# Expert layers of a four-layer kernel: gate maximum and difference in the step of the transposes, gates in seven steps

## Chip, cores and metric

The kernel runs on 1 core of one Trainium2 chip. The metric is the device time of one execution in microseconds (us), lower is better. Before the change it is 4801.95 us, the median of 3 runs (4800.6 to 4808.87).

## What is computed

A tensor of 4 images with 128 channels and 64 x 64 positions passes four layers: a deformable convolution, a state-space block, a layer of attention and feed-forward with experts behind it, and a second attention, again with experts behind it. The change touches the experts alone, which occur twice with the same code. Seen as tokens, the input is 16,384 rows of 128 numbers; each row chooses 2 of 8 experts:

```python
def _ln_t(v, eps=1e-5):
    m = jnp.mean(v, axis=-1, keepdims=True)
    s = jnp.var(v, axis=-1, keepdims=True)
    return (v - m) / jnp.sqrt(s + eps)

def _L2_ffn_ref(x, router_w, router_b, expert_w, expert_b):
    B, N, D, C, E, K = (8, 8192, 128, 128, 8, 2)
    router_probs = jax.nn.softmax(x @ router_w + router_b, axis=-1)
    top_p, top_i = jax.lax.top_k(router_probs, K)
    top_p = top_p / jnp.sum(top_p, axis=-1, keepdims=True)
    expert_out = jnp.einsum('bnd,edc->bnec', x, expert_w) + expert_b
    gathered = jnp.take_along_axis(expert_out, top_i[..., None], axis=2)
    return jnp.einsum('bnk,bnkc->bnc', top_p, gathered)

t = t + _L2_ffn_ref(_ln_t(t), ...)     # layer 2, behind its attention
...
t = t + _L3_ffn_ref(_ln_t(t), ...)     # layer 3, the same with other weights
x = _from_tokens(t, x)
```

The kernel computes all 8 experts for every row and weighs them with a gate that is zero for 6 of the 8.

## The kernel before

`moe(layer)` (line 2063) is one expert layer. All 16,384 rows lie in SBUF as `X`, seen as `T`: 128 tiles of 128 rows by 128 channels. The tiles are taken in nine groups, `SIZES = [8, 8] + [16] * 7`. A group passes four stages, each written as a generator that stops at a `yield` after each step:

- `moments(i)` (line 2101): one BN_STATS on VectorE per tile into the PSUM tile `w`, then seven small operations on `odd`, `rstd` and `w`; ScalarE makes `rstd` from them by Ln and Exp; VectorE makes `mean`.
- `logits(i)` (line 2126): ScalarE writes the normalised tiles `v`; four at a time are transposed by TensorE into the PSUM bank `psv`, copied by ScalarE into `vT`, and multiplied by the router weights into `psl`; at the end ScalarE copies `psl` into `lT`.
- `gates(i)` (line 2157): TensorE transposes `lT` into the PSUM bank `psg` (four transposes); VectorE takes the maximum `m` over the 8 logits of a row and writes the difference into `both`; ScalarE takes Exp of `both`; VectorE does the rest on `both`, `w` (the work space for `pr` and `one`), `mx`, `rk`, `m` and ends with `gate`. In the profile the parts of this rest are: "m<-both, reciprocal, w<-both,w, mx<-w" (four operations), twice "w<-w,mx; w<-w,rank; rk<-w; w<-w,rk" (four operations each, called the match below), between them "gate<-w; w<-w,gate; both<-w,mx; mx<-w" (the removal), and at the end five operations that end with `gate<-w,m`.
- `experts(i, s)` (line 2210), one pair of tiles per call: per tile two products of TensorE into two banks `pex` (four per pair; the profile counts each as two passes), scaled by the gate and added up. In even slots ScalarE scales three experts per tile and VectorE the other five (`x<-pex,gate` and `x<-pex,gate,x`); in odd slots ScalarE scales four and VectorE four (`x<-pex,gate`, 128 x 512). GpSimd adds what is left (`x<-x`) and adds the sum onto `X`.

`flip(q)` (line 2235), in layer 3 alone, transposes four finished tiles by TensorE into the bank `psf`, ScalarE copies them into `o`, and SP's queue sends `o` to the output.

`psv`, `psg` and `psf` share one PSUM buffer: the pool `pv` has `bufs=1` and all three have `tag="psv"`. `pex` has five buffers, `x` three.

The rounds `p = -3 ... 8` (line 2247) run the four stages in a skewed way: round `p` computes the experts of group `p` in slots of one pair, and beside it the gates of `p+1`, the logits of `p+2` and the moments of `p+3`. Rounds -3 to -1 have no experts and 12 slots, rounds 0 and 1 have 4 slots, rounds 2 to 8 have 8. In each slot `experts` is issued first, then in layer 3 after each second pair a `flip`, then steps of the gates, the logits and the moments, in that order, as many as the share of the round that has passed asks for:

```python
for step, i in ((gates, p + 1), (logits, p + 2), (moments, p + 3)):
    if 0 <= i < N:
        parts = {gates: 8, logits: SIZES[i] // 2 + 2, moments: SIZES[i] // 4 + 3}[step]
        beside.append([step(i), parts, 0])
...
    for a in beside:
        while a[2] < -(-a[1] * (s + 1) // slots):
            next(a[0])
            a[2] += 1
```

`moe` issues through `InOrder`, which holds every engine to this order of the program; every instruction issued through it carries line 85 in the profile. With 8 slots, one gates step falls on each slot. With 4 slots, two fall on each. With 16 tiles in a group of the logits and 8 slots, the first four `v` are written in slot 0, the first transposes into `psv` come in slot 1.

Of the kernel before, what the change touches and what calls it, by code (L numbers as in the profile page):

```python
# [94 lines left out]
class Kernel:  # L95
# [1967 lines left out]
    def moe(self, layer):  # L2063
# [6 lines left out]
        SIZES = [8, 8] + [16] * 7  # L2070
        T = self.X.rearrange("p (t c) -> p t c", c=P)
        LAST = P - 1
        with ExitStack() as ctx:
# [83 lines left out]
            def gates(i):  # L2157
                n = SIZES[i]
                vT, lT = st.pop(("logits", i))
                ps = pv.tile([P, 4, 4, 32], F32, name="psg", tag="psv")  # L2160
                for k in range(4):
                    nc.tensor.transpose(ps[:, k].rearrange("p j e -> p (j e)"), lT[:, k * P:(k + 1) * P], self.ident)
                quads = [P, n // 4, 4, NE]
                sh = [P, n, NE]
                psl = ps[:, :, 0:n // 4, 0:NE].rearrange("p k j e -> p j k e")

                def across(x):
                    return x.unsqueeze(2).to_broadcast(sh)

                yield  # L2170

                pr, one = (work[name][:, 0:n] for name in ("pr", "one"))
                both = sm.tile(sh, F32, name=f"both{n}")
                gate = sm.tile(sh, F32, name=f"gate{n}")
                m = sm.tile([P, n], F32, name=f"m{n}")
                mq = m.rearrange("p (j k) -> p j k", k=4)
                nc.vector.tensor_reduce(mq, psl, AX.X, ALU.max)
                nc.vector.tensor_tensor(both.rearrange("p (j k) e -> p j k e", k=4), psl,
                                        mq.unsqueeze(3).to_broadcast(quads), ALU.subtract)
                yield  # L2180
                nc.scalar.activation(both, both, AF.Exp)
                yield
                nc.vector.tensor_reduce(m, both, AX.X, ALU.add)
                nc.vector.reciprocal(work["m"][:, 0:n], m)
                nc.vector.tensor_tensor(pr, both, across(work["m"][:, 0:n]), ALU.mult)

                mx = sm.tile([P, n, 2], F32, name=f"mx{n}")
                rk = sm.tile([P, n], F32, name=f"rk{n}")
                for k in range(2):
                    nc.vector.tensor_reduce(mx[:, :, k], pr, AX.X, ALU.max)  # L2190
                    yield
                    nc.vector.tensor_tensor(one, pr, across(mx[:, :, k]), ALU.is_equal)
                    nc.vector.tensor_tensor(one, one, rank.unsqueeze(1).to_broadcast(sh), ALU.mult)
                    nc.vector.tensor_reduce(rk, one, AX.X, ALU.max)
                    nc.vector.tensor_tensor(one, one, across(rk), ALU.is_equal)
                    yield
                    if k == 0:
                        nc.vector.tensor_scalar(gate, one, -2.0, None, ALU.mult)
                        nc.vector.tensor_add(pr, pr, gate)
                        nc.vector.tensor_tensor(both, one, across(mx[:, :, 0]), ALU.mult)  # L2200
                    else:
                        nc.vector.tensor_tensor(one, one, across(mx[:, :, 1]), ALU.mult)
                        nc.vector.tensor_add(one, one, both)
                nc.vector.tensor_reduce(m, mx, AX.X, ALU.add)
                nc.vector.reciprocal(m, m)
                nc.vector.tensor_tensor(gate, one, across(m), ALU.mult)
                st["gates", i] = vT, gate
                yield

            def experts(i, s):  # L2210
                vT, gate = st["gates", i]
                t0 = first[i] + 2 * s
                x = xp.tile([P, 2, NE, P], F32, name="x")
                at_once = s % 2 == 0
                for u in range(2):
                    k = 2 * s + u
                    pex = [pe.tile([P, 4, P], F32, name="pex") for h in range(2)]
                    for h in range(2):
                        nc.tensor.matmul(pex[h], vT[:, k, :], ew[:, 512 * h:512 * (h + 1)], start=True, stop=True)
                    for e in range(3 if at_once else 4):  # L2220
                        nc.scalar.activation(x[:, u, e, :], pex[0][:, e, :], AF.Identity, scale=gate[:, k, e:e + 1])
                    if at_once:
                        nc.vector.tensor_scalar(x[:, u, 3, :], pex[0][:, 3, :], gate[:, k, 3:4], None, ALU.mult)
                        for e in range(4):
                            nc.vector.scalar_tensor_tensor(x[:, u, e, :], pex[1][:, e, :],
                                                           gate[:, k, 4 + e:5 + e], x[:, u, e, :],
                                                           ALU.mult, ALU.add)
                    else:
                        nc.vector.tensor_tensor(x[:, u, 4:NE, :], pex[1],
                                                gate[:, k, 4:NE].unsqueeze(2).to_broadcast([P, 4, P]), ALU.mult)  # L2230
                for w in (2, 1) if at_once else (4, 2, 1):
                    nc.gpsimd.tensor_tensor(x[:, :, 0:w, :], x[:, :, 0:w, :], x[:, :, w:2 * w, :], ALU.add)
                nc.gpsimd.tensor_tensor(T[:, t0:t0 + 2, :], T[:, t0:t0 + 2, :], x[:, :, 0, :], ALU.add)

            def flip(q):

                ps = pv.tile([P, 512], F32, name="psf", tag="psv")
                for k in range(4):
                    nc.tensor.transpose(ps[:, k * P:(k + 1) * P], T[:, 4 * q + k, :], self.ident)
                o = xp.tile([P, 512], F32, name="o")  # L2240
                nc.scalar.copy(o, ps)
                n, q = divmod(q, L // 512)
                nc.sync.dma_start(self.out[n][:, q * 512:(q + 1) * 512], o)
# [3 lines left out]
            for p in range(-3, N):  # L2247

                beside = []
                for step, i in ((gates, p + 1), (logits, p + 2), (moments, p + 3)):  # L2250
                    if 0 <= i < N:
                        parts = {gates: 8, logits: SIZES[i] // 2 + 2, moments: SIZES[i] // 4 + 3}[step]
                        beside.append([step(i), parts, 0])
                slots = SIZES[p] // 2 if p >= 0 else 12
                for s in range(slots):
                    if p >= 0:
                        experts(p, s)
                        pairs += 1
                        if layer == 3 and pairs % 2 == 0 and pairs >= 6:
                            flip(pairs // 2 - 3)  # L2260
# [5 lines that stand above are left out]
                    assert next(a[0], None) is None and a[2] == a[1]  # L2266
# [705 lines left out]
```

## Time and profile before

| view | value |
|---|---|
| profiled execution, its own time | 4802.76 us |
| span of that execution | 4800.9 us |
| median of the 3 runs | 4801.95 us |
| busy share of the span: PE, DVE, ACT, POOL | 92%, 71%, 75%, 65% |
| experts of layer 2, first BN_STATS to last add onto `X` | 2196.91 to 2513.5 us |
| experts of layer 3, first BN_STATS to the end | 4458.26 to 4800.9 us |
| 2340 to 2360 us (layer 2, a middle round): PE, DVE, ACT, POOL busy of 20 us | 18.60, 15.34, 14.30, 18.25 |
| 4620 to 4640 us (layer 3, a middle round): the same | 17.93, 14.77, 14.51, 16.13 |
| 2200 to 2220 us and 4460 to 4480 us (starts): PE busy of 20 us, granted clock | 13.67 at 0.50; 12.34 at 0.53 |
| a round of 8 slots, from one `psg` to the next | 34.69 us in layer 2, 37.38 us in layer 3 |

A line of the timeline gives start, duration, engine, operation, what it writes and reads, how many instructions were merged, and in brackets how long the engine had been idle before and what ended that. Times are from the start of the span. The whole kernel has 67,063 instructions; the two expert layers take 317 and 343 us of it.

### The profile page before, as it was taken

The page shows a single profiled execution, that of the slowest core. Times are in us where ns is not written, and L with a number is a line of the kernel's source. Part 1 is how long each engine was busy: PE and PEld are TensorE (multiplying, and loading weights), DVE is VectorE, ACT ScalarE, POOL GpSimd, SP SyncE. Part 2 cuts the span into 40 slices and gives each one's busy share as a digit, 9 for nine tenths or more (in the row PEclk, how much of TensorE's full clock was granted, in tenths as well). Part 3 has the DMA queues.
Part 4 walks back from the last instruction along what each step waited for, and adds up shares of the span by engine and source line. Part 5 has one row for each costly group of instructions (what it writes and reads, how often), then busy time and mean ns, then how long its engine had stood idle before and what let it go on. Part 6 is the DMA issues. An engine that isn't in the chain of part 4 may idle for free. (4 is left out here: it accounts for less than half of the span.)

```text
span 4800.9 us, 67063 instructions
## 1 busy us (share of the span) xinstructions
PE 4424.1 (92%) x23064; PEld 2411.2 (50%) x23064; DVE 3391.4 (71%) x6475; ACT 3618.5 (75%) x5498; POOL 3117.7 (65%) x3443
## 2 busy tenths in 40 slices
PE   6889987899997899997989999999999999999798
PEld 4778775566774344443434444444444444444344
DVE  5999996666645888855866666766676666665675
ACT  4456553566666777775758999999999999999575
POOL 0234443367783455544887878887888788877488
PEclk9999999999998999998999999999999999999899
DMA  6666773101002000000000000000000000000000
GB/s 213 186 184 188 194 193 82 26 22 30 28 17 90 23 1 1 0 1 1 36 36 1 1 1 1 1 1 1 1 1 1 1 1 1 1 1 1 10 29 34
DMA packets 71704, 196.33 MB, mean 41 GB/s; under 512 B 13940, under 2 KB 17204, under 8 KB 69684
## 3 DMA queue, kind: packets, MB, share of 16 engines
q1 hardware_dynamic: 65924, 175.96, 12.8%
q0 software_dynamic: 2240, 12.85, 1.0%
q8 instruction: 187, 3.06, 0.3%
q10 hardware_dynamic: 3184, 3.08, 0.2%
q14 instruction: 169, 1.38, 0.1%
HBM read 133.23 MB, written 50.74 MB: 38 GB/s over the span
## 5 line engine op out<-in xcount | busy, mean ns | idle before, releaser
L85 POOL TENSOR_TENSOR r<-r 128x512 f32<-128x512 f32 (+1 forms) x1088 | 1348.7, 1241 | 332.4 <-DVE r L85 271.8
L85 DVE TENSOR_TENSOR r<-r,num 128x1024 f32<-128x1024 f32 (+1 forms) x1088 | 975.4, 928 | 599.6 <-PE num L85 495.2
L85 PE MATMUL D<-F,G 32*128 32x512 f32 (+3 forms) x4608 | 1139.2, 573 | 2.1 <-DVE den L85 0.9
L85 PE MATMUL num<-F,G 32*128 32x512 f32 (+3 forms) x4608 | 1057.2, 590 | 6.8 <-DVE r L85 3.9
L85 ACT ACTIVATE r<-r 128x2048 f32<-128x2048 f32 (+4 forms) x610 | 1018.5, 1679 | 51.3 <-POOL r L85 4.7
L85 ACT ACTIVATE r<-D 128x1536 f32<-128x1536 f32 (+1 forms) x544 | 763.6, 1404 | 49.8 <-PE D L85 29.6
L85 PEld LDWEIGHTS D<-F,G 32*128 32x128 f32 x4608 | 484.2, 184 | 373.6 <-issue 235.1
L85 PE MATMUL acc<-r,v 128*128 128x512 f32 (+3 forms) x1152 | 598.1, 606 | 0.7 <-ACT r L85 0.7
L85 POOL TENSOR_TENSOR x<-x 128x512 f32<-128x512 f32 (+2 forms) x320 | 405.4, 1267 | 148.4 <-DVE m L85 66.5
L85 PEld LDWEIGHTS num<-F,G 32*128 32x128 f32 x4608 | 383.3, 183 | 223.4 <-issue 110.7
L85 PE MATMUL pff<-hid,w_ffn_w2T 128*128 128x512 f32 x1024 | 468.6, 600 | 0.0
L85 PE MATMUL pex<-w_expert_w,vT 128*128 128x512 f32 x1024 | 461.4, 598 | 1.6 <-DVE x L85 1.4
L85 POOL TENSOR_TENSOR piece<-v,wt 128x512 f32<-128x512 f32 x160 | 167.6, 1065 | 376.2 <-DVE cum L85 90.0
L85 PEld LDWEIGHTS acc<-r,v 128*128 128x128 f32 x1152 | 174.1, 188 | 382.7 <-issue 180.4
L85 PE MATMUL acc<-ident,pr 128*128 128x128 f32 x2560 | 319.1, 282 | 45.2 <-DVE pr L85 45.2
L85 ACT ACTIVATE x<-pex,gate 128x128 f32<-128x128 f32 x896 | 257.5, 368 | 102.2 <-PE pex L85 76.9
L85 PEld LDWEIGHTS acc<-ident,pr 128*128 128x128 f32 x2560 | 296.0, 146 | 59.9 <-DVE pr L85 58.6
L85 ACT ACTIVATE hid<-phh,cols 128x512 f32<-128x512 f32 x416 | 253.1, 689 | 67.7 <-PE phh L85 67.7
L85 PEld LDWEIGHTS pex<-w_expert_w,vT 128*128 128x128 f32 x1024 | 190.6, 192 | 216.5 <-issue 160.6
L85 PEld LDWEIGHTS pff<-hid,w_ffn_w2T 128*128 128x128 f32 x1024 | 185.0, 191 | 200.9 <-issue 200.9
L85 DVE TENSOR_TENSOR pr<-v,near_w 128x2560 f32<-128x2560 f32 x96 | 270.2, 2815 | 6.2 <-PE acc L85 5.4
L85 DVE SCALAR_TENSOR_TENSOR cop<-lp,cols,cop 128x512 f32<-128x512 f32 x192 | 143.4, 747 | 35.5 <-ACT cop L85 33.4
(502 smaller groups left out, 7656.6 us busy)
## 6 DMA issues: line engine op xcount, KB each, us to landing
v<-tab SPq DMA_DIRECT2D x320, 256.0 KB
oms<-omw SPq DMA_DIRECT2D x32, 432.0 KB
omr<-oms SPq DMA_DIRECT2D x32, 432.0 KB
X<-in_x_dram SPq DMA_DIRECT2D x8, 1024.0 KB
tab<-vb SPq DMA_DIRECT2D x64, 128.0 KB
o<-o SPq DMA_DIRECT2D x32, 256.0 KB
oin<-o SPq DMA_DIRECT2D x32, 256.0 KB
kept<-X SPq DMA_DIRECT2D x4, 2048.0 KB
```

The source lines that it names most:

```text
L85: self.last = op(*args, **kwargs)
```

## The change

The first `yield` of `gates` goes, the one between the transposes into `psg` and the tiles of the next step. The first step of the gates now issues the four transposes, the maximum and the difference; the second is the Exp, and so on, seven steps in all. The number in the table of parts is set to 7.

```diff
@@ -2167,8 +2167,6 @@
                 def across(x):
                     return x.unsqueeze(2).to_broadcast(sh)
 
-                yield
-
                 pr, one = (work[name][:, 0:n] for name in ("pr", "one"))
                 both = sm.tile(sh, F32, name=f"both{n}")
                 gate = sm.tile(sh, F32, name=f"gate{n}")
@@ -2249,7 +2247,7 @@
                 beside = []
                 for step, i in ((gates, p + 1), (logits, p + 2), (moments, p + 3)):
                     if 0 <= i < N:
-                        parts = {gates: 8, logits: SIZES[i] // 2 + 2, moments: SIZES[i] // 4 + 3}[step]
+                        parts = {gates: 7, logits: SIZES[i] // 2 + 2, moments: SIZES[i] // 4 + 3}[step]
                         beside.append([step(i), parts, 0])
                 slots = SIZES[p] // 2 if p >= 0 else 12
                 for s in range(slots):
```

No instruction is added or removed. With 8 slots the seven steps fall on slots 0 to 6, one each. With 4 slots two fall on each of the slots 0 to 2 and one on slot 3. With 12 slots they fall on slots 0, 1, 3, 5, 6, 8 and 10, where the eight steps fell on 0, 1, 3, 4, 6, 7, 9 and 10.

## Prediction

> **What bounds the kernel now.** First the engines' shares of the span: PE is busy for 92%, and in the middle rounds of both expert layers for 18 of 20 us, so there the question is what makes PE pause. The chain of waits of layer 3 tells it (start, duration, what the end hung on):
>
> ```profile
> 4616.80 3.45 PE pex L85 x8
> ...
> 4620.27 0.69 DVE x L85
> 4620.96 0.21 DVE m L85
> ...
> 4621.19 0.30 DVE both L85
> ...
> 4621.63 0.65 PE psf L85 x4
> ```
>
> The chain leaves PE for one scaling, the maximum and the difference. PE's timeline shows why, here for layer 3 and, in the last line, layer 2:
>
> ```profile
> 4616.19 0.60 PE L85 MATMUL psg<-ident,lT 128*128 128x128 f32 x4
> 4616.63 3.60 PE L85 MATMUL pex<-w_expert_w,vT 128*128 128x512 f32 x8
> 4621.63 0.63 PE L85 MATMUL psf<-ident,X 128*128 128x128 f32 x4 [1.40 <-DVE both L85]
> 4622.94 0.66 PE L85 MATMUL psv<-ident,v 128*128 128x128 f32 x4 [0.68 <-ACT o L85]
> ...
> 2313.39 0.63 PE L85 MATMUL psv<-ident,v 128*128 128x128 f32 x4 [1.40 <-DVE both L85]
> ```
>
> `psf` (layer 3) or `psv` (layer 2) wants the one buffer that holds `psg` until DVE has read it in slot 1, behind slot 1's scaling. This happens five times in layer 2 (rounds 2 to 6; round 7 has no logits) and six times in layer 3 (rounds 2 to 7), always 1.40 us.
>
> Then what lies close behind PE: POOL's timeline in an 8-slot round of layer 2, and its last pauses in each layer.
>
> ```profile
> 2319.03 2.07 POOL L85 TENSOR_TENSOR x<-x 128x512 f32<-128x512 f32 x2 [0.87 <-DVE x L85]
> ...
> 2331.22 4.50 POOL L85 TENSOR_TENSOR x<-x 128x1024 f32<-128x1024 f32 x3 [1.15 <-DVE x L85]
> ...
> 4739.37 2.07 POOL L85 TENSOR_TENSOR x<-x 128x512 f32<-128x512 f32 x2 [0.85 <-DVE x L85]
> ```
>
> POOL has 0.87 + 1.15 = 2.0 us to spare in a round of 34.69 us. Last the timelines of DVE, ACT and PE in the starts and the rounds of 4 slots, whose order the change also moves:
>
> ```profile
> 4468.03 1.31 DVE L85 BATCH_NORM_STATS2 w<-X 128x6 f32<-128x128 f32 x4
> 4473.38 0.23 DVE L85 TENSOR_REDUCE m<-psg 128x8 f32<-128x64 f32 x1 [4.05 <-PE psg L85]
> 4484.06 0.22 DVE L85 TENSOR_TENSOR gate<-w,m 128x64 f32<-128x64 f32 x1
> 4484.38 1.66 ACT L85 ACTIVATE x<-pex,gate 128x128 f32<-128x128 f32 x6 [2.32 <-PE psg L85]
> 4488.51 0.63 PE L85 MATMUL psv<-ident,v 128*128 128x128 f32 x4 [4.13 <-DVE both L85]
> 4488.97 5.29 PE L85 MATMUL pex<-w_expert_w,vT 128*128 128x512 f32 x8
> ...
> 2241.10 0.31 ACT L85 ACTIVATE rstd<-rstd,eps 128x16 f32<-128x16 f32 x1 [1.41 <-DVE rstd L85]
> 2244.25 1.13 PE L85 MATMUL psl<-vT,rws 128*128 128x512 f32 x2 [2.00 <-ACT vT L85]
> ```
>
> Both lie on the path: at the start PE waits 4.13 us for what hangs on `gate`, and at the end of a 4-slot round PE waits 2.00 us for a chain DVE statistics, ACT `rstd`, `v`, `vT`.
>
> **The 8-slot rounds: the gain.** The maximum and difference move to slot 0, behind slot 0's scalings. In layer 3 DVE's work of slot 0 ends at 4617.74 and `psg` is there at 4616.79: no new wait. The buffer is free while PE does the 3.60 us of slot 1, so all pauses go: 11 x 1.40 = 15.4 us. The copy of `o` (0.68) still holds `psv` once.
>
> What is late next: POOL. In layer 2 its spare 2.0 us takes the 1.40 of each round, except that in round 2 slot 5's `x` comes only 0.6 us earlier and POOL passes on the other 0.8; POOL's last pause (1.15 us at 2435.28) is used up and it runs through to the end. In layer 3 its last pause is the 0.85 us of the fence above, against 1.40: 0.55 is given back. Net gain 15.4 - 0.8 - 0.55 = 14.05.
>
> The rest of the gates come one slot earlier each, over the same instructions: four operations (1.25 us) go into slot 2, the match (four operations, 1.32) out of slot 7. PE gets its `pex` banks back from DVE later in between; the tightest bank has 0.65 us left by my replay of slot 6. I cost it at nothing; if that cover is gone, a pause as long as the lost one comes back.
>
> **The starts: four statistics.** In round -1 four BN_STATS lie ahead of `m<-psg`, inside its wait of 4.05 us. They now come behind it, and DVE then runs without a pause up to `gate`, so `gate` comes 1.31 us later, in two layers: +2.6. The bounds are 0 (another pause takes them) and 3.0 (Exp ahead of two `v` adds 0.2 each).
>
> **Slot 0 of the 4-slot rounds: Exp ahead of the four `v`.** Two gates steps fall on a slot. Before they were transposes and maximum; now maximum and Exp. ACT's Exp waits for DVE's `both`, and the four `v` (1.66 for four) queue behind it on ACT. `psv` needs both the buffer and the `v`; before, the `v` were written during the wait for `both`. So if `both` ends at B, the next `pex` started at B + 0.61 (0.14 from the chain, 0.47 from `psv` to `pex` in the fence). Now the Exp (I take 0.31, as for the small ACT operation `rstd`) and the four `v` (1.66) come first, each transposed as it is written, and some 0.13 for the last: B + 2.1. That is +1.5 in each of four rounds, 6.0, less 0.57 in layer 3 round 1, where `m<-both` waited so long for the Exp: +5.4. Bounds: 0 if the chain at the end of the round keeps its time, 4 x 1.97 = 7.9 if Exp and `v` come wholly on top.
>
> **Slots 0 to 3 of the same rounds: one match more ahead of the statistics.** The seven small operations that lead to `rstd` stand behind the gates' steps in DVE's queue. With seven steps one more match is ahead of them: 4 x 0.26 = 1.05 (128 x 64) in round 0, 1.32 (128 x 128) in round 1. The chain behind it (Ln and Exp, `x` of slot 3, `vT`, `psl`, the next round's `psg`) moves by it: 2 x 2.37 = +4.7. Bounds 0 to 4.7.
>
> Sum of the losses 2.6 + 5.4 + 4.7 = 12.7 (12.8 unrounded); with the gain, -1.3.
>
> **The granted clock.** Pauses cost more than their length. After 4.13 us PE's next eight passes took 5.29 instead of 3.60: 1.7 us for one stretch at half clock. It also came after 2.64 + 0.68 us (1.06 + 0.48 = 1.54), and once out of eleven after 1.40 + 0.68:
>
> ```profile
> 4546.99 8.73 PE L85 MATMUL pex<-w_expert_w,vT 128*128 128x512 f32 x16
> ```
>
> where five other rounds show 7.03. It did not come after 1.88, 2.00, 1.71 and 2.73. The change lengthens six such pauses of rounds 0 and 1: in slot 0 1.88, 1.71 and 1.72 to some 3.2 to 3.75, in slot 3 2.00, 1.99 and 2.73 to some 3.05, 3.04 and 4.05. I take half of them slow, 3 x 1.7 = 5.1, and drop the stretch of 4546.99, whose first pause goes: +3.4. Bounds: none slow, -1.7; all slow, 10.2 - 1.7 = +8.5.
>
> [...]
>
> **The sum.** The profiled execution took 4802.76 us (span 4800.9 and 1.86 around it), 0.8 above the median of the runs. 4802.76 - 14.05 + 12.8 + 3.4 = 4804.9, less 0.8: 4804. With the clock's bounds and half of the uncertain losses it is 4797 to 4811.
>
> **Rivals.**
>
> A, faster. The gain is paid eleven times from measured pauses; the losses are argued. If the ends of the 4-slot rounds absorb all that slot 0 and the starts lose, only the gain is left: 4801.95 - 14.05 = 4788; with half absorbed (6.4) and the clock unchanged 4794 to 4796. For it: in a 4-slot round PE also waits for that chain, and one of two delays on parallel paths costs nothing. Against: DVE feeds both paths and is late in both.
>
> B, all six lengthened pauses run into half clock: 4804 + 5.1 = 4809, and 4813 with the long pauses at the starts' slots costing one more stretch in each layer. For it: the stretch after 1.40 + 0.68. Against: none after 2.73.
>
> C, slower. One mechanism: the 1.25 us that go from slot 3 to slot 2 make DVE late with its scalings in slots 2 to 6, banks of `pex` come back late, and PE's pause returns there. It decides once DVE is more than 0.65 us later than worked out; then the 15.4 us stay and the losses come on top: 4802 + 12.8 + 3.4 to 4.0 = 4818 to 4819. For it: five banks for pairs of four. Against: DVE is busy for only 14.8 to 15.3 of 20 us there, and the same operations fill slots 3 to 7 today without a pause of PE.
>
> D, the change does not do what it says: the scheduler holds the order of the program, so the maximum does move to slot 0. If its wait on `psg` cost as much as it saves, 4802.
>
> **How the numbers follow.** The measurement tells 0.2% apart, 9.6 us: faster is below 4792.3, slower above 4811.6. Chances: the forecast .48, A .18, B .14, C .18, D .02. Most of the forecast, half of B and D lie within the bound: .46 + .07 + .02, and about .05 of A (half absorbed) makes .60 the same. Faster is A's other .13 and .01 of the forecast's edge, .14; slower is C .18, B .07 and .01 of the edge, .26. The likeliest is the forecast, 4804. To leave out 2 in 10, 4792 (most of A below it) to 4817 (C above it).
>
> **What would show it.** In the changed profile the eleven pauses of 1.40 "<-DVE both" are gone and a round of 8 slots takes 33.3 us in layer 2 and 36.0 in layer 3 (right), or pauses of `pex` stand in slots 4 to 6 (C). At the starts DVE has its four BN_STATS behind `both` and `gate` lies 1.3 later. In rounds 0 and 1 `psv` is released by ACT's `v` about 1.5 later, the waits of `psl` are longer by 1.05 and 1.32 (if they are as before, A), and eight passes of 5.3 instead of 3.60 count the stretches at half clock. The forecast is wrong by most if the two delays of a 4-slot round overlap.

## The result, and the profile after

The changed kernel takes 4810.14 us (median of 20 runs, 4807.57 to 4813.54); before it is 4802.64 us (20 runs, 4799.69 to 4810.84). The ratio is 1.0013, 95% interval 1.0007 to 1.0019: 3.4 to 9.1 us slower. That is inside the 0.2% that the prediction called no change, and inside its range, but on the losing side of its 4804.

The gain arrived whole. The chain of waits in a middle round of layer 3 of the changed kernel (start, duration, what the end hung on) goes from `pex` to `psf` without DVE:

```profile
4630.02 0.44 PE psg L85 x4
4630.45 3.44 PE pex L85 x8
4633.89 0.45 PE psf L85 x4
...
4634.36 0.59 ACT o L85
...
4635.00 0.66 PE psv L85 x4
```

PE's timeline shows the same for layer 2, and DVE's timeline (layer 3) that the maximum and the difference are done while PE works on slot 1:

```profile
2289.28 0.60 PE L85 MATMUL psg<-ident,lT 128*128 128x128 f32 x4
2289.72 3.60 PE L85 MATMUL pex<-w_expert_w,vT 128*128 128x512 f32 x8
2293.15 0.60 PE L85 MATMUL psv<-ident,v 128*128 128x128 f32 x4
...
4631.42 0.28 DVE L85 TENSOR_REDUCE m<-psg 128x16 f32<-128x128 f32 x1
4631.73 0.29 DVE L85 TENSOR_TENSOR both<-psg,m 128x128 f32<-128x128 f32 x1
```

From `pex` to `psv` it is 3.43 us where it was 5.00 (2273.70 to 2278.70 before): not 1.40 but 1.57. The profile lets the eight passes end 3.60 us after their start, but without a pause the next instruction starts after 3.43; that overlap of 0.17 is lost beside the idle time. `psv` behind a pause takes 0.03 longer (0.63, otherwise 0.60), so a round gains 1.59. A round of 8 slots takes 33.10 in place of 34.69 us in layer 2, and 35.78 in place of 37.37 in layer 3.

The loss stands in the rounds of 4 slots. Before, PE's timeline showed at the start of round 0 in layer 2:

```profile
2227.12 0.63 PE L85 MATMUL psv<-ident,v 128*128 128x128 f32 x4 [1.88 <-DVE both L85]
2227.59 3.60 PE L85 MATMUL pex<-w_expert_w,vT 128*128 128x512 f32 x8
```

After, in rounds 0 and 1 of layer 2:

```profile
2231.76 1.62 PE L85 MATMUL psv<-ident,v 128*128 128x128 f32 x4 [3.52 <-ACT v L85]
2233.18 4.80 PE L85 MATMUL pex<-w_expert_w,vT 128*128 128x512 f32 x8
...
2252.23 1.69 PE L85 MATMUL psl<-vT,rws 128*128 128x512 f32 x2 [3.33 <-ACT vT L85]
2253.71 4.77 PE L85 MATMUL pex<-w_expert_w,vT 128*128 128x512 f32 x8
...
2261.27 1.48 PE L85 MATMUL psv<-ident,v 128*128 128x128 f32 x4 [2.35 <-ACT v L85]
2262.59 5.30 PE L85 MATMUL pex<-w_expert_w,vT 128*128 128x512 f32 x8
...
2283.19 1.93 PE L85 MATMUL psl<-vT,rws 128*128 128x512 f32 x2 [4.38 <-ACT vT L85]
2284.91 4.53 PE L85 MATMUL pex<-w_expert_w,vT 128*128 128x512 f32 x8
```

Four pauses are released by ACT's `v` and `vT`, two in each round, and after every one the eight passes take 4.5 to 5.3 us instead of the 3.60 of before; the granted clock over them is 0.67 to 0.79, where it was 1.00. ACT's timeline of round 0 names what ACT was stopped by: Exp of `both` ahead of the four `v`, and `rstd` ahead of `x` and `vT`.

```profile
2231.07 0.26 ACT L85 ACTIVATE both<-both 128x64 f32<-128x64 f32 x1 [2.35 <-DVE both L85]
2231.23 1.63 ACT L85 ACTIVATE v<-X,mean,rstd 128x127 f32<-128x127 f32 x4
...
2249.08 0.31 ACT L85 ACTIVATE rstd<-rstd,eps 128x16 f32<-128x16 f32 x1 [2.75 <-DVE rstd L85]
2249.42 0.21 ACT L85 ACTIVATE rstd<-rstd 128x16 f32<-128x16 f32 x1
2249.54 2.16 ACT L85 ACTIVATE x<-pex,gate 128x128 f32<-128x128 f32 x8
2251.54 0.63 ACT L85 COPY vT<-psv 128x512 f32<-128x512 f32 x1
```

The table holds, for every profile taken, the time from one `psg` to the next in the rounds of 4 slots, and the two expert layers together (from a layer's first `psv` to the first `D<-ident` behind it in layer 2, to the end of the span in layer 3). The layers' sum leaves out what the earlier stages scatter: the rest of the span was 4147.7 to 4159.1 us over these profiles.

| kernel | layer 2 round 0 | round 1 | layer 3 round 0 | round 1 | both layers | median of runs |
|---|---|---|---|---|---|---|
| before | 24.00 | 24.62 | 27.96 | 28.03 | 652.6 | 4802.64 |
| before, second profile | 24.16 | 26.32 | 24.34 | 29.60 | 652.5 | |
| changed | 30.68 | 30.96 | 32.67 | 33.56 | 656.6 | 4810.14 |
| changed, second profile | 30.69 | 30.96 | 32.82 | 33.57 | 656.8 | |
| new order in 8-slot rounds alone | 24.00 | 24.63 | 30.70 | 28.32 | 634.3 | 4787.74 |
| new order in 4-slot rounds alone | 30.08 | 30.54 | 30.23 | 33.61 | 672.7 | 4821.78 |
| 8-slot and Exp early | 27.32 | 27.80 | 31.17 | 30.87 | 643.7 | 4796.60 |
| 8-slot and match early | 26.87 | 27.77 | 31.81 | 30.44 | 643.4 | 4796.66 |
| 8-slot and start | 26.67 | 24.61 | 27.07 | 29.63 | 639.7 | 4790.28 |
| changed, PE kept busy | 29.00 | 29.25 | 31.14 | 31.86 | 650.1 | 4802.40 |
| 8-slot, `rstd` late | 22.87 | 22.56 | 26.63 | 24.00 | 625.5 | 4776.86 |
| changed, `rstd` late | 26.34 | 23.86 | 28.36 | 25.28 | 632.3 | 4784.83 |
| 8-slot, `rstd` late, `psv` later | 21.55 | 21.55 | 22.89 | 23.55 | 618.8 | 4771.90 |

### The profile page after: what moved, and what is told of

It is laid out like the page before. It is cut to its first block, busy times and chain, and to the rows that moved or that the text cites. A ratio compares the mean times of both kernels' runs of the same rounds, so it can differ in the third digit from the quotient of the medians.

```text
span 4808.9 us, 67066 instructions
## 1 busy us (share of the span) xinstructions
PE 4437.1 (92%) x23064; PEld 2420.5 (50%) x23064; DVE 3390.2 (70%) x6475; ACT 3620.0 (75%) x5498; POOL 3119.1 (65%) x3443
```

## The experiments

All edits are to the changed kernel. Most need a hand-written number of steps per slot in the rounds of 4 slots; that part is shown once, with the first experiment.

**The new order in the rounds of 8 slots alone.**

```diff
+                if i == 0:
+                    yield
                 pr, one = (work[name][:, 0:n] for name in ("pr", "one"))
...
+                four = {gates: (1, 3, 5, 7)}
...
-                        parts = {gates: 7, logits: SIZES[i] // 2 + 2, moments: SIZES[i] // 4 + 3}[step]
-                        beside.append([step(i), parts, 0])
+                        parts = {gates: 7 + (i == 0), logits: SIZES[i] // 2 + 2, moments: SIZES[i] // 4 + 3}[step]
+                        beside.append([step(i), parts, 0, four.get(step) if p in (0, 1) else None])
...
-                        while a[2] < -(-a[1] * (s + 1) // slots):
+                        while a[2] < (a[3][s] if a[3] else -(-a[1] * (s + 1) // slots)):
```

> The changed kernel, but in the start (round -1) and the two rounds of 4 slots the steps of the gates fall on their old slots; only the rounds of 8 slots have the new order. Theory (the loss lies in the start and the 4-slot rounds, and is added to a full gain): eleven pauses of 1.40 go, and as the changed profile's rounds are 1.59 shorter, not 1.40, the gain is 16.8, and 18.5 with the slow stretch of layer 3 round 2: 4784 to 4787, faster than before by 0.3 to 0.4%. Rival (the gain itself is smaller, the shorter rounds of the profile being one execution's): 4792 to 4797.

4787.74 against 4802.70 us, ratio 0.9966 (0.9952 to 0.9980); the layers are 18.3 us shorter. By its profile the gain is whole and agrees with the theory. The median alone, 15.0 us, lies between theory and rival, and its interval reaches both.

**The new order in the rounds of 4 slots alone.**

```diff
+                if i not in (1, 2):
+                    yield
...
-                        parts = {gates: 7, logits: SIZES[i] // 2 + 2, moments: SIZES[i] // 4 + 3}[step]
+                        parts = {gates: 7 + (i not in (1, 2)), logits: SIZES[i] // 2 + 2, moments: SIZES[i] // 4 + 3}[step]
```

> The kernel before, but with the new order of the gates in the two rounds of 4 slots of each layer; start and 8-slot rounds as before. Theory (delays add up on one path, each lengthened pause is followed by a stretch at half clock): 6.7 + 6.3 in layer 2 and 4.7 + 5.5 in layer 3, as in the changed profile, less about 2 for the start: +21, 4823. Rival (the delays add up, the clock does not matter): 4 x 1.5 + 4.6 = +10.6, 4813. Rival A of the prediction (two delays on parallel paths hide each other): at most +6, 4808.

4821.78 us, ratio 1.0036 (1.0023 to 1.0050), the layers 20.1 longer. Delays that hide each other (4808) are out, and so is a price without the clock (4813, a ratio of 1.0021).

**8-slot rounds, and the Exp alone early**, as the first experiment but `gates: (2, 3, 5, 7)`.

> As the run with the new order in the 8-slot rounds alone (-17), and in the 4-slot rounds the Exp alone is moved into slot 0, ahead of the four v; the matches stay in their old slots. Theory with the clock: 4 x 1.5 and three new slow stretches of 1.7: -17 + 11 = -6, 4797. Theory without the clock: -17 + 6 = -11, 4792. If the Exp costs nothing: 4785. In its profile the first psv of the 4-slot rounds is released by ACT's v, and the psl at the end of the round waits as before (2.0 and 2.7).

4796.60 us, ratio 0.9984 (0.9975 to 0.9993). The median is the theory's, though its interval takes in the 4792 without the clock; the profile decides: the first `psv` is released by ACT's `v` in all four rounds, the first eight passes behind it take 5.29, 5.29 and 5.30 us in the three that were at full speed before, and the end of the round in layer 2 waits 2.15 and 2.93, little more than the 2.0 and 2.7 of before.

**8-slot rounds, and one match early**, `gates: (1, 4, 6, 7)`.

> As the run with the new order in the 8-slot rounds alone (-17), and in the 4-slot rounds the Exp stays in slot 1, but one match more stands ahead of the seven statistics. Theory with the clock: +4.6 and three slow stretches of 1.7 (layer 3 round 1 is slow there already): -17 + 9.7 = -7, 4795. Theory without the clock: -17 + 4.6, 4790. If the match costs nothing: 4785. In its profile the waits of psl at the end of the 4-slot rounds are longer by 1.05 and 1.32, and the first psv waits for DVE's both as before (1.88, 1.71).

4796.66 us, ratio 0.9986 (0.9977 to 0.9995); `psl` waits 3.18 in round 0 and 4.17 in round 1 of layer 2, `psv` 1.87 and 1.71 as before. Stretches of half clock follow both waits in layer 2 (eight passes of 5.29 and 4.93 us), none the 3.18 of layer 3 (3.60). The match cost, on top of its length, what the clock made of it, some 1.7 us behind each of those two.

**8-slot rounds and the start**, `gates: (1, 3, 5, 7)` and the `yield` for `i == 0` left out.

> As the run with the new order in the 8-slot rounds alone (-17), and the start has the new order too; the 4-slot rounds keep the old one. Theory: gate 1.1 to 1.3 later in each layer, +2.6, and +1.7 if the longer pause in slot 0 of layer 2 falls to half clock: -12.7 to -14.4, 4788 to 4790. If the four statistics cost nothing: 4785.

4790.28 us, ratio 0.9974 (0.9963 to 0.9984): 2.5 above the first experiment by the medians, as the four statistics were priced; the interval doesn't exclude nothing. By the profile layer 2's first pause is 2.86 instead of 1.88, with a slow stretch behind it (eight passes of 5.29 us).

The parts add up roughly to the change. Rounds of 8 slots, Exp, match and start, by the medians: -15.0 + 8.9 + 8.9 + 2.5 = +5.3, against the change's own +7.5 (3.4 to 9.1); by the layers -18.3 + 9.4 + 9.1 + 5.4 = +5.6, against +4.0 and +4.3.

**PE kept busy in the pauses.** The transposes are repeated into the same bank with the same values:

```diff
+                    again = 6 if h == n // 4 - 1 and (i == 2 or i == 3 and layer == 2) else 1
-                    for k in range(4):
+                    for k in [k for _ in range(again) for k in range(4)]:
                         nc.tensor.transpose(ps[:, k * P:(k + 1) * P], v[:, 4 * h + k, :], self.ident)
...
-                for k in range(4):
+                for k in [k for _ in range({1: 5, 2: 3}.get(i, 1)) for k in range(4)]:
                     nc.tensor.transpose(ps[:, k].rearrange("p j e -> p (j e)"), lT[:, k * P:(k + 1) * P], self.ident)
```

> The changed kernel, whose PE repeats transposes into the same bank during the long pauses of the start and the 4-slot rounds (the four transposes into psg five times for round 0, three times for round 1; the last four into psv six times, not for layer 3 round 1). The result is the same, the waits are the same; only PE is not idle. Theory (the 1.7 us after each long pause is PE's clock, and idleness brings it): about 6 us go in layer 2 and 3 to 5 in layer 3: 4799 to 4801, some 10 below the changed kernel. Rival (the passes are long for want of something else, banks or weights, or the clock falls whatever PE does): 4810 or above.

4802.40 us, ratio 0.9998 (0.9989 to 1.0007); the layers are 6.5 below the changed kernel's, where 9 to 11 were expected. In each of the four rounds one slow stretch of about 1.7 went (30.68 to 29.00, 30.96 to 29.25, 32.67 to 31.14, 33.56 to 31.86) and one stayed. PE's timeline of layer 3 round 1, with the repeated transposes:

```profile
4526.56 1.47 PE L85 MATMUL psg<-ident,lT 128*128 128x128 f32 x12
4529.51 1.48 PE L85 MATMUL psv<-ident,v 128*128 128x128 f32 x4 [1.47 <-ACT v L85]
4530.82 3.60 PE L85 MATMUL pex<-w_expert_w,vT 128*128 128x512 f32 x8
```

ACT's `v` releases the same `psv`, which takes the same 1.48 us, yet the passes take 3.60. The table of windows (busy time and count of PE, PEld, DVE, ACT and POOL, then the granted clock, the share and rate of the DMA) shows 3.5 us behind that point, first for the changed kernel,

```profile
4529.00:4532.50 3.50, 3.50 (x6) 1.52 (x6) 0.55 (x3) 2.50 (x7) 0.33 (x1) 0.55 0.02 5
```

then with PE kept busy:

```profile
4531.00:4534.50 3.50, 3.50 (x11) 1.54 (x11) 1.02 (x3) 3.29 (x11) 0.15 (x1) 1.00 0.00 0
```

The clock is 0.55 there and 1.00 here, with 6 and 11 matmuls in the same time. So the long passes go with the granted clock, and in this pair the clock goes with PE's idleness ahead: behind the repeated transposes the same `psv` has 1.47 us of idle time in front of it in place of 2.35. That the stretches which went did not go by chance is shown in the last section.

**8-slot rounds, `rstd` late**, as the first experiment with

```diff
-                four = {gates: (1, 3, 5, 7)}
+                four = {gates: (1, 3, 5, 7), moments: (2, 4, 5, 7)}
```

> As the run with the new order in the 8-slot rounds alone, and in the 4-slot rounds Ln and Exp of rstd go from slot 2 to slot 3, behind the copies of vT and lT on ACT. Theory (at the end of a 4-slot round PE waits only because ACT is stopped by rstd, with x, vT and psl queued behind it): the pauses of 2.00, 2.73, 1.99 and 2.64 fall to about 0.7, 6.5 us, and 1.5 for the slow stretch of layer 3 round 1: 8 below that run, 4777. Rival (the statistics are needed at once: the v of the next round come late and the wait moves to slot 0): 4785 or above.

4776.86 us, ratio 0.9943 (0.9929 to 0.9957). ACT's timeline at the end of round 0 of layer 2, with PE's product between:

```profile
2246.01 0.59 ACT L85 COPY vT<-psv 128x512 f32<-128x512 f32 x1 [0.55 <-PE psv L85]
2246.65 1.12 PE L85 MATMUL psl<-vT,rws 128*128 128x512 f32 x2 [0.68 <-ACT vT L85]
2247.81 0.59 ACT L85 COPY lT<-psl 128x512 f32<-128x512 f32 x1 [1.22 <-PE psl L85]
2248.29 0.31 ACT L85 ACTIVATE rstd<-rstd,eps 128x16 f32<-128x16 f32 x1
```

`vT` is no longer behind `rstd`, and the pause of 2.00 is 0.68; the later `rstd` is not missed in the next round, whose first pause is 1.71 us as before.

**The changed kernel with `rstd` late**, `four = {moments: (2, 4, 5, 7)}` alone.

> The changed kernel with Ln and Exp of rstd behind the copies of vT and lT in slot 3 of the 4-slot rounds. Theory: the extra match ahead of the statistics costs nothing any more, nor do the slow stretches after it (4.6 + 5), and the old waits of psl shrink as well (6.5 + 1.5); the Exp ahead of v still costs: 4810 - 17 = 4793, 4790 to 4800 with the bounds. Rival (the statistics chain is needed in the next round as it is): 4808 to 4812.

4784.83 us, ratio 0.9962 (0.9948 to 0.9976): below the 4790 to 4800 expected. The direction is the theory's, but the effect was larger than expected: the waits of 3.33, 4.38 and 3.33 fell to 0.68 each and the 3.62 went (12.6 us), all four slow stretches behind them went (6.8), and so did the two behind the 2.35 of round 1 (3.4), which I had left in. The 2.5 us of the start and the early Exp remain, 8 above the run before this.

**`psv` later as well**, in the run with `rstd` late in the 8-slot order:

```diff
-                four = {gates: (1, 3, 5, 7), moments: (2, 4, 5, 7)}
+                four = {gates: (1, 3, 5, 7), moments: (2, 4, 5, 7), logits: (2, 5, 8, 10)}
```

> As the run with Ln and Exp of rstd moved into slot 3, and in the 4-slot rounds the first transposes into psv go from slot 0 to slot 1, behind slot 1's products. Theory (PE pauses in slot 0 only because psv is queued ahead of products that need nothing of it): the pauses of 1.88 (2.06) and 1.71 go in layer 2, 1.72 in layer 3 round 1, each with 0.19 of refill, and 0.68 behind psv comes in their place: 4 below that run's 4777, 4773. Rival (psv and its copies crowd slot 1, and the banks of pex come back late there): 4777 or above.

4771.90 against 4801.39 us, ratio 0.9937 (0.9924 to 0.9951), by the median the fastest version here and near the theory's 4773. The interval alone does not exclude the rival's 4777; the layers are 6.7 us shorter than in the run without the later `psv`, which fits the theory. No pause above 1.1 us is left in PE's rounds of 4 slots.

**Both kernels profiled again.**

> The kernel before, unchanged, for a second profile. The two expert layers took 315.3 and 337.3 us in the first. If their time is the same from execution to execution, it is 652 to 653 again, and only the stages ahead of them scatter; if the slow stretch of layer 3 round 2 is chance, 651.

> The changed kernel, unchanged, for a second profile. The two expert layers took 320.5 and 336.1 us in the first, 4.0 more than before, where the medians differ by 7.5. If the layers account for all of the difference, they take 658 to 660 here; if the rest is scatter of other stages, 656 to 657 again.

The layers take 652.5 us again before and 656.8 after the change. The difference of 4.0 to 4.3 is the same in both pairs; the remaining 3 of the median's 7.5 lies outside the expert layers, where the instructions are the same, and inside the scatter of those stages. Whether any of it is real stays open; the interval (from 3.4) holds the layers' number.

## Why the prediction was off where it was

**The gain** was priced at 15.4 less 1.35. The runs showed 11 x 1.59 = 17.5, as a pause cost PE 0.19 us beside its idle time of 1.40. POOL gave back nothing in layer 2 and 0.7 in layer 3. Its timeline, two pauses of layer 2 and the last of layer 3:

```profile
2344.32 4.50 POOL L85 TENSOR_TENSOR x<-x 128x1024 f32<-128x1024 f32 x3 [0.58 <-ACT v L85]
...
2443.34 4.50 POOL L85 TENSOR_TENSOR x<-x 128x1024 f32<-128x1024 f32 x3 [0.36 <-DVE x L85]
...
4742.10 4.50 POOL L85 TENSOR_TENSOR x<-x 128x1024 f32<-128x1024 f32 x3 [0.30 <-DVE x L85]
```

POOL still pauses once in every round of layer 2 in the faster kernel, so the 0.8 that it was to pass on there was wrong, and the 33.1 us are PE's own: its timeline shows no pause there.

**DVE late in slots 2 to 6** (rival C, the work moved there costed at nothing) did not come: PE shows no pause of `pex` in rounds 2 to 7.

**The losses without the clock** were 12.8 by the sum. From the table's rounds, read pause by pause against before: in layer 2 start and Exp 2.75, match 1.17, Exp 1.50, match 1.46; in layer 3 2.28, 1.20, 1.48 and 0.79; together 12.6. Rival A's parallel paths don't exist: both delays lie on DVE, then ACT, then PE, one behind the other, and the two single experiments add up (8.9 and 8.9 by the medians, against 19.1 with both and without the gain).

**The granted clock is the step that failed**: "I take half of them slow". All six of the lengthened pauses were followed by half clock, in both profiles of the changed kernel (eight passes of 4.53 to 5.30 us behind each), so the term is not 3.4 but 8.1 us in the first profile: 6.3 in layer 2; in layer 3 1.2 and 3.3 in the rounds of 4 slots, less 1.7 for the stretch of round 2 that went and 0.95 at its start. The mechanism was rival B's, which had a chance of .14. With the larger gain it comes to -16.8 + 12.6 + 8.1 = +3.9, the layers' +4.0. Gain and clock were both priced too low, by 2.8 and 4.7 us, and these errors partly cancel; that the measured time stayed inside the range is in part luck.

Why it failed can be read from all profiles together. I had compared PE's idle times, by which 2.64 + 0.68 was slow and 2.73 was not (and 1.40 + 0.68 stood six times in layer 3, not eleven times). The pauses of slot 0 that I put at 3.2 to 3.75 came as 3.52 once and 2.35 twice, because PE starts `psv` on the first `v` (at 2231.76 in round 0, while ACT writes the four from 2231.23 to 2232.86): `psv` takes 1.62 and 1.48 in place of 0.63. What tells more than the idle time is the stop: the time from 0.43 us after the start of the last pass of one 128 x 512 product (`pex` or `psl`), where the next instruction could have started (eight passes more make 7.03 us of 3.60, 0.43 each), to the start of the next such product. The 128 x 128 transposes in between are part of it. The profile draws the last pass 0.16 longer, so by the lines a stop looks 0.16 shorter. In layer 2 from 2222 us on and in layer 3 from 4483 us on, over twelve profiles (the one with repeated transposes left out), the stops that began at full clock were:

| stop, us | cases | half clock behind it |
|---|---|---|
| 1.7 to 3.3 | 92 | 0 |
| 3.3 to 3.4 | 19 | 2 |
| 3.4 to 4.3 | 24 | 19 |
| above 4.3 | 21 | 21 |

By this count the "2.00" of before was a stop of 2.6, the 2.73 one of 3.32, the 1.40 + 0.68 of layer 3 one of 3.36, and the 2.64 + 0.68 one of 4.13; the change made 3.93, 4.27, 4.98 and 5.54 of the four in layer 2, and 3.93 and 4.26 of the two in layer 3. The length alone does not decide. The 2.73 went the other way in the second profile of before, with the same wait. The first profile:

```profile
2268.87 1.13 PE L85 MATMUL psl<-vT,rws 128*128 128x512 f32 x2 [2.73 <-ACT vT L85]
2269.84 3.60 PE L85 MATMUL pex<-w_expert_w,vT 128*128 128x512 f32 x8
```

and the second:

```profile
2271.11 1.12 PE L85 MATMUL psl<-vT,rws 128*128 128x512 f32 x2 [2.72 <-ACT vT L85]
2272.07 5.29 PE L85 MATMUL pex<-w_expert_w,vT 128*128 128x512 f32 x8
```

In that second profile the stretch of layer 3's round 2 did not come either (37.37 in place of 39.07), so the 1.7 that I dropped for it was chance and not part of the change.

What went with it in these profiles is how the stop fell on a grid. In every one of the thirteen profiles the granted clock is either 1.00 or 0.50, and it changes only at instants that are multiples of 3.41 us apart. The table of windows on that grid (PE's busy time and count, the clock, the share and rate of the DMA) shows the same wait, in the first profile of before

```profile
2263.51:2266.92 3.41, 2.64 (x10) 1.00 0.00 0
2266.92:2270.34 3.42, 1.47 (x4) 1.00 0.00 0
```

and in the second:

```profile
2268.86:2272.27 3.41, 1.16 (x3) 1.00 0.00 0
2272.27:2275.68 3.41, 3.41 (x5) 0.50 0.00 0
```

In the first 1.95 of the 2.73 us of waiting fall in one window; in the second 2.25 of the 2.72 do, and the next window runs at half clock. Over all thirteen profiles, in both layers as above up to the last `pex`, I count PE's work in each window that ran at full clock, 0.43 us for a pass and 0.11 for a transpose (four of `psg` take 0.44 to the start of `pex`). All 46 windows with at most 1.41 us of work were followed by half clock, and none of the 2056 with 1.46 or more. Where PE was busy all through, the stretch lasted one window and cost half of it, 1.7 us (5.30 for eight passes in place of 3.60). So "half of them" had no ground, but "all six" is not certain either: with the new order in the rounds of 4 slots alone, the 2.35 of layer 2's round 1 kept the full clock and the other five did not.

The place of the grid against the kernel differs between executions, here by 0.30 us for the same `psl` in the two profiles of before. The window ahead of a slow stretch need not be empty: up to 1.41 us of work in it did not keep the clock. That of the 1.40 + 0.68 held 1.03 us of work; that of the 2.64 + 0.68 held no product, and only 0.5 us of transposes.

## What to carry to other kernels

When steps of one stage are drawn together, look at the shortest rounds of the schedule first: a step that falls one slot earlier there may put an instruction that waits (here Exp and `rstd` on ACT) ahead of those that another engine is hungry for; what is gained eleven times in long rounds was lost in four short ones, and keeping the old places there and in the start was worth 22 us (4810.14 to 4787.74). Where an engine is held to the program's order, as ACT is here, an instruction that waits belongs behind the copies that feed the bounding engine (with `rstd` behind `vT` a pause of 2.00 us became 0.68). A pause of PE is to be measured from one wide product to the next: up to 3.3 us it never cost the clock here, above 4.3 us it always did, another 1.7 us, and in between it hung on where the windows of 3.41 us fell.

## What the hardware showed beside that

Transposes of 128 x 128 went with a kept clock too: with 8 to 20 more of them in the stop, four stops of 3.9 to 4.26 us all kept the full clock (19 of 24 lost it without). Their windows on the grid held only 0.33 to 0.65 us of products, but 1.8 to 2.1 us of work with the transposes; in the other profiles every window with so few products was followed by half clock, so where the grid fell does not explain it. Three stops of 4.97, 5.56 and 8.8 us lost the clock all the same: each left a window with 1.06, 1.24 and 0.42 us of work.

And equal stops differ by the grid: 4.26 us behind the same 2.35 us of waiting gave half clock in both layers of the changed kernel, where a window was left with 0.98 and 1.02 us of work, and full clock in both layers once `rstd` was late, where the emptiest windows held 1.70 and 1.68. Why the grid falls where it does against the kernel was not tried.
